# A two-layer graph kernel whose edge loops run 5 iterations of 500 groups in place of 25 iterations of 100

## The chip, the cores and the metric

The kernel runs on one core of one Trainium2 chip. The metric is the device time in microseconds (us); lower is better. The time given for the kernel before is the median of three runs. A profile is one further execution, recorded instruction by instruction; it is slower than the timed runs, and its own time is given beside theirs.

The engines are named as the profile names them: PE (matrix multiplies, with PEld for its weight loads), DVE (vector), ACT (scalar activations and copies), POOL (here almost only the issuing of indirect DMAs), SP (issues plain DMAs).

## What is computed

There are 30,000 nodes of 128 numbers and 960,000 edges, sorted by destination. Layer 0 normalises the nodes, then applies two relational graph convolutions with 32 edge types made of 8 basis matrices; layer 1 normalises again and applies a gated convolution with 4 edge types.

```python
h = relu(layernorm(x))                      # layer 0
def rel_graph_conv(h, basis, coeff, bias):  # W_r = sum_b coeff[r, b] * basis[b]
    msg = (h @ W)[src, etype32] * edge_weight
    return segment_sum(msg, dst) + bias
x = x + rel_graph_conv(relu(rel_graph_conv(h, 1)), 2)

h = relu(layernorm(x))                      # layer 1
for t in range(4):
    k, q, v = h @ Wk[t] + bk[t], h @ Wq[t] + bq[t], h @ Wv[t] + bv[t]
    msg = where(etype4 == t, sigmoid(k[dst] + q[src]) * v[src], 0)
    outs[t] = segment_sum(msg, dst) + h @ Ws[t] + b[t]
x = x + mean(outs)
```

## The kernel before

**Preparation (lines 187 to 290).** Twenty-five steps of 1,200 nodes (`STEPS`) compute `h0`, the normalised nodes. `load(i)` fetches rows on SP; `statistics(i)` takes ten means and variances on DVE, then the square root on ACT and, back on DVE, the reciprocal and the shift; `results(i)` applies them in ten ACT instructions and stores. In the loop (lines 266 to 270) the statistics of step i+1 stand ahead of the results of step i. Between them goes one piece of `edge_chunk`, which turns destinations into positions within a window and looks for positions out of range; `even` and `late` (lines 280 to 286) test that the edges of a group do not reach nodes that a node step has yet to finish. If anything fails, `any_path`, a general and unsorted version, is run instead of `sorted_path`.

**Three passes over the edges (`edge_pass`, lines 342 to 381).** `c1` and `c2` are the two relational convolutions (`rel_body`), `g` is the gated one (`gate_body`). The unit of work is a group of 384 edges (G = 3 tiles of 128), whose destinations fall into a window of 32 nodes; S = 5 groups are a step; SB = 5 steps share one set of index loads (`loads(k)`), whose number per iteration is NQ. There are 2,500 groups. `NI` iterations of `NG` groups, 25 of 100, are the turns of a hardware loop; the body of an iteration is written out in full. The loop is of the kind "staggered": the engines do not meet at its end but may run on into the next stage, and the body is cut by `tc.stage_boundary()` into four stages (every 25 groups), with `leave_stage()` two steps into each one.

**A group of `c1` and `c2`.** POOL issues three indirect gathers (line 118, called in line 523), each of 128 rows, into `hg`, which has five buffers: POOL can be five groups, 15 gathers, ahead of PE. DVE makes `hits` once a step and `sb` once a group (line 527). PE multiplies `hg` by `sb` into `pa` (line 531) and ACT copies `pa` into `ab` (line 535). After a step `bases_out` (line 486) multiplies `ab` by the eight basis matrices into `pb`, and `add_windows` (line 414) adds the result to the resident array `agg` on DVE, two steps later. In `c1` the coefficients come from `types`, `onehot` (line 451 on DVE, line 456 on PE) and `coefficients` (line 466), which are made two steps and one step ahead; the first ones of an iteration are made at its start, before its first group (lines 496 to 500), and the last two steps are finished after its last group (lines 549 to 551).

**A group of `g`.** POOL gathers three tiles into `qv` (ten buffers: 30 gathers ahead), PE looks up keys by a one-hot product into `pk` (line 588), DVE adds, ACT takes the sigmoid, DVE multiplies (`msg`, line 597), PE sums into `po` (line 599).

**Node steps (`after_first`, `after_second`, `after_third`).** When all edges of 120 nodes (VB) are done, these nodes are finished: activation, transposes, store; in `after_second` also the normalisation and the products with 12 weight matrices. A node step is a list of pairs (n, piece); step u of an iteration places a piece at group u * PERIOD + n, where `beside(n)` runs it after the group's own instructions. PERIOD is 9 before, so the pieces move by one place within the five groups of a step from one node step to the next. LAG = 480 nodes are not yet finished when the loop ends; four node steps after each pass, interleaved, finish them (lines 375 to 381).

**Codes.** In `c1`, once an iteration, `codes` (lines 785 to 815) computes the indices that pass `g` will use: four loads on SP, three DVE instructions, two stores on ACT.

The order of instructions on each engine is the order of the program text; nothing is rearranged.

Of the kernel before, what the change touches and what calls it, by code (L numbers as in the profile page):

```python
# [9 lines left out]
F32 = mybir.dt.float32  # L10
I32 = mybir.dt.int32
BF16 = mybir.dt.bfloat16
# [23 lines left out]
NGR = NT // G  # L36
S = 5
SB = 5
NQ = 4
NS = NQ * SB  # L40
NGS = S * SB
NTS = NGS * G
NG = S * NS
# [1 line left out]
NI = NGR // NG  # L45
VB = 120
NPI = N // NI
PERIOD = NG * VB // NPI - 1
LAG = 4 * VB
NX = N + LAG  # L50
LEAD = 3 * VB
GAP = 8
EPS = 1e-5
CH = 5
# [18 lines left out]
def kernel(  # L73
# [113 lines left out]
    with tc.tile_pool(name="prep", bufs=2) as prep, tc.tile_pool(name="pre", bufs=4) as pre, \  # L187
# [37 lines left out]

        def load(i):
            if i < STEPS:
                xts[i] = pre.tile([PX, KX, D], F32, name="xt")
                nc.sync.dma_start(xts[i], rows(x, i))

        def statistics(i):
            if i < STEPS:
                st = pre.tile([PX, KX, 6], F32, name="st")
                mvs[i] = pre.tile([PX, KX, 2], F32, name="mv")
                for k in range(KX):
                    nc.vector.bn_stats(st[:, k, :], xts[i][:, k, :])
                    nc.vector.bn_aggr(mvs[i][:, k, :], st[:, k, :])
                scales[i] = pre.tile([PX, KX], F32, name="rs")
                nc.scalar.activation(scales[i], mvs[i][:, :, 1], AF.Sqrt, bias=eps[:PX])
                nc.vector.reciprocal(scales[i], scales[i])  # L240
                shifts[i] = pre.tile([PX, KX], F32, name="off")
                nc.vector.scalar_tensor_tensor(shifts[i], mvs[i][:, :, 0], -1.0, scales[i],
                                               op0=ALU.mult, op1=ALU.mult)

        def results(i):
            h = pre.tile([PX, KX, D], F32, name="h")
            for k in range(KX):
                nc.scalar.activation(h[:, k, :], xts[i][:, k, :], AF.Relu,
                                     scale=scales[i][:, k:k + 1], bias=shifts[i][:, k:k + 1])
            nc.scalar.dma_start(rows(h0, i), h)  # L250
# [9 lines left out]

        with tc.manual_schedule():
            between = edge_steps()
            for i in range(3):
                load(i)
            statistics(0)
            for i in range(STEPS):
                load(i + 3)
                statistics(i + 1)
                next(between, int)()
                results(i)  # L270
            for step_ in between:
                step_()
# [62 lines left out]
    def sorted_path():  # L335

        for u in range(NPI // VB):
            late = min(g for g in range(NG)
                       if min((g // S + 2) * S + S - 2, NG) > u * PERIOD + 1)
            assert (u + 1) * VB - late * NPI // NG <= LEAD  # L340
        with ExitStack() as all_:
            def edge_pass(name, body, after, banks, extra=None):


                with ExitStack() as held:
                    weights = held.enter_context(tc.tile_pool(name=f"{name}_w", bufs=1))
                    steps, start = after(weights), body(weights)
                    with tc.tile_pool(name=f"{name}_io", bufs=NQ) as io, \
                            tc.tile_pool(name=f"{name}", bufs=2) as pool, \
                            tc.tile_pool(name=f"{name}_n", bufs=1) as npool, \  # L350
                            tc.tile_pool(name=f"{name}_nps", bufs=banks, space=PSUM) as nps, \
                            tc.tile_pool(name=f"{name}_c", bufs=1, space=PSUM) as cps, \
                            tc.tile_pool(name=f"{name}_ps", bufs=2, space=PSUM) as ps:
                        cp = cps.tile([P, 4 * D], F32, name="cp")
                        iw, ic = cp[:, :W], cp[:, W:W + 1]
                        nc.vector.tensor_copy(iw, irow)
                        nc.vector.tensor_copy(ic, icol)
                        run = start(cps)
                        with tc.For_i(0, NI, 1, iteration_sync="staggered") as i:
                            with tc.manual_schedule():  # L360
                                todo = {}
                                for n, step_ in extra(i, npool) if extra else ():
                                    todo.setdefault(n, []).append(step_)
                                for u in range(NPI // VB):
                                    at = i * -NPI + (N + LAG - (u + 1) * VB)
                                    for n, step in steps(at, npool, nps, 2):
                                        todo.setdefault(u * PERIOD + n, []).append(step)
                                assert W < TQ * 8 * B and max(todo) < NG

                                def beside(n):  # L370
                                    for step in todo.get(n, ()):
                                        step()

                                run(i, io, pool, ps, cp, iw, ic, beside)
                    left = LAG // VB
                    with tc.tile_pool(name=f"{name}_l", bufs=left) as lpool, \
                            tc.tile_pool(name=f"{name}_lps", bufs=8, space=PSUM) as lps:
                        for together in zip(*(steps(at, lpool, lps, left)
                                              for at in range(0, LAG, VB))):
                            for _, step in together:  # L380
                                step()
# [34 lines left out]
            def rel_body(table, weights, second):  # L416
# [13 lines left out]
                def body(bas, pos, hits, i, io, pool, ps, cp, iw, ic, beside):  # L430
# [70 lines left out]
                    for s in range(NS):  # L501
                        k = s // SB
                        if s % SB == 0:
                            if s:
                                tc.stage_boundary()
                            if k + 1 < NQ:
                                loads(k + 1)
                        if s % SB == 2:
                            leave_stage()
                        idx, relc, start = stage[k][:3]  # L510
                        if s + 2 < NS:
# [42 lines left out]
            def gate_body(i, io, pool, ps, cp, iw, ic, beside):  # L554
# [54 lines left out]
                for n in range(NG):  # L609
                    s, g, k = n // S, n % S, n // NGS  # L610
                    if n % NGS == 0:
                        if n:
                            tc.stage_boundary()
                        if k + 1 < NQ:
                            loads(k + 1)
                    if g == 0 and s % SB == 2:
                        leave_stage()
                    if g == 0 and s + 1 < NS:
                        types(s + 1)
# [56 lines left out]
            def after_second(weights):  # L676
# [9 lines left out]
                def steps(at, pool, ps, deep):  # L686
# [63 lines left out]
                    def own():  # L750
                        nc.vector.scalar_tensor_tensor(cols, xs, bsc, got["po"], op0=ALU.add,
                                                       op1=ALU.add)

                    return ((1, copy), (2, rows_), (3, stats), (4, norm_), (5, turn), (6, relu),
                            (7, weight(0)), (7, weight(1)),
                            (8, biased(0, kt)), (8, biased(1, qvt[:, :, :D])),
                            (8, weight(2)), (8, part),
                            (9, biased(2, qvt[:, :, D:])), (9, own), (9, store(knode, kt)),
                            (10, store(qvnode, qvt)))
                return steps  # L760

            def after_third(weights):
# [21 lines left out]

            def codes(i, pool):

                dr, er, kr = (pool.tile([NG, GE], t, name=n) for n, t in (
                    ("dr", I32), ("er_row", I32), ("kr", F32)))
                kc = pool.tile([NG, GE], BF16, name="kc")
                sx, ex = (pool.tile([TP, NQ * NTS], I32, name=n) for n in ("sx", "ex"))  # L790
                cols = ds(i * (NQ * NTS), NQ * NTS)

                def rows(array):
                    return bass.AP(tensor=array.tensor, offset=i * (NG * GE),
                                   ap=[[GE, NG], [1, GE]])

                def load():
                    nc.sync.dma_start(dr, rows(dst_row))
                    nc.sync.dma_start(er, rows(et4_row))
                    nc.sync.dma_start(sx, src[:, cols])  # L800
                    nc.sync.dma_start(ex, et4[:, cols])

                def less():
                    nc.vector.tensor_tensor(kr, dr, dr[:, 0:1].to_broadcast([NG, GE]),
                                            ALU.subtract)
                    nc.vector.scalar_tensor_tensor(sx, sx, float(T), ex, op0=ALU.mult, op1=ALU.add)

                def typed():
                    nc.vector.scalar_tensor_tensor(kc, kr, float(T), er, op0=ALU.mult, op1=ALU.add)

                def store():
                    nc.scalar.dma_start(rows(kcode), kc)
                    nc.scalar.dma_start(qidx[:, cols], sx)

                return (NGS + 1, load), (NGS + 6, less), (NGS + 7, typed), (NGS + 8, store)

            edge_pass("c1", rel_body(h0, basis[0], False), after_first, 2, codes)
            edge_pass("c2", rel_body(h1, basis[1], True), after_second, 2)
# [233 lines left out]
```

## Time and profile before

| | us |
|---|---|
| median of three timed runs (28445.0 to 28455.75) | 28447.31 |
| time of the profiled execution | 33838.86 |
| its span, first to last instruction | 33837.1 |
| POOL busy in it | 21296.4 |
| PE busy | 19734.2 |
| PE weight loads busy | 16782.1 |
| DVE busy | 11542.2 |
| ACT busy | 3644.4 |

In the profiled execution the first gather of `c1` starts at 169.48 us, that of `c2` at 11314.35, that of `g` at 22339.68, and the last one of all at 33805.12. The mean granted clock of PE is 0.681 of full speed over the span. A line of the profile's list of groups reads: line of the code, engine, operation, output and inputs, count, then the busy time in us and the mean ns of one, then the idle time of the engine just ahead of these instructions and what ended it. A line of a timeline reads: start in us, length in us, engine, line, operation, and in brackets the idle time before it and what ended that.

### The profile page before, as it was taken

What the parts mean: (1) busy time and instruction counts of PE and PEld (TensorE: products, weight loads), DVE (VectorE), ACT (ScalarE), POOL (GpSimd) and SP (SyncE); (2) the same over time, 40 slices, a digit from 0 to 9 for tenths busy, and PEclk for the clock granted to TensorE, in tenths of its full rate; (3) what the DMA queues carried; (4) which work ended last, traced back from release to release, by engine and by line L of the source; (5) the groups of instructions that cost most, each with busy time, mean ns of one, the idle gap of its engine ahead of it and who ended that gap; (6) DMA issues with size and microseconds to landing.
All of it is one profiled execution on the core that took longest, in us unless ns stands there. A gap on an engine that the chain in (4) does not pass through costs nothing.

```text
span 33837.1 us, 297715 instructions
## 1 busy us (share of the span) xinstructions
PE 19734.2 (58%) x83304; PEld 16782.1 (50%) x83304; DVE 11542.2 (34%) x23695; ACT 3644.4 (11%) x9834; POOL 21296.4 (63%) x22514
## 2 busy tenths in 40 slices
PE   4555555555555555665566565655555555555555
PEld 3444444444444444444444444445555555555555
DVE  3333333333333333333333333333333333333333
ACT  1000000000000111111111111111111111111111
POOL 5666666666666666666666666666666666666665
PEclk8777777777777777777777777765555555555555
DMA  3222222222222222222222222234444444444444
GB/s 102 66 65 64 65 64 66 65 65 65 65 65 64 65 65 66 66 65 65 65 65 66 65 65 65 65 103 124 124 124 124 124 124 125 124 124 124 125 124 120
DMA packets 1973054, 2913.52 MB, mean 86 GB/s; under 512 B 678765, under 2 KB 1355881, under 8 KB 1971545
## 3 DMA queue, kind: packets, MB, share of 16 engines
q0 software_dynamic: 840000, 1967.52, 21.4%
q1 hardware_dynamic: 725347, 651.17, 6.4%
q10 hardware_dynamic: 406197, 276.11, 2.9%
q8 instruction: 777, 12.73, 0.2%
q14 instruction: 733, 6.00, 0.1%
HBM read 2618.79 MB, written 274.16 MB: 85 GB/s over the span
## 4 chain that ended last, share of the span: by engine, by line


## 5 line engine op out<-in xcount | busy, mean ns | idle before, releaser
L118 POOL DMA_INDIRECT hg<-h,idx x15000 | 14175.6, 945 | 8092.4 <-issue 4258.4
L531 PE MATMUL pa<-sb,hg 128*128 128x256 f32 x30000 | 9232.2, 464 | 6808.7 <-issue 5685.1
L531 PEld LDWEIGHTS pa<-sb,hg 128*128 128x128 f32 x30000 | 6848.7, 238 | 8712.6 <-issue 6423.5
L118 POOL DMA_INDIRECT qv<-qvtab,qi x7500 | 7093.9, 946 | 4416.4 <-issue 2291.4
L599 PE MATMUL po<-sel,msg 128*128 128x32 f32 x15000 | 3449.8, 386 | 4592.3 <-DVE msg L597 3790.8
L599 PEld LDWEIGHTS po<-sel,msg 128*128 128x128 f32 x15000 | 3410.6, 327 | 4881.1 <-DVE msg L597 3957.9
L527 DVE TENSOR_TENSOR sb<-hits,ce 128x768 f32<-128x768 f32 x5000 | 4597.1, 949 | 541.7 <-issue 221.1
L588 PE MATMUL pk<-kw,oh 128*128 128x128 f32 x15000 | 3960.9, 437 | 183.7 <-issue 160.3
L535 ACT COPY ab<-pa 128x256 f32<-128x256 f32 x5000 | 1811.3, 373 | 19679.2 <-remote 9114.6
L629 DVE TENSOR_TENSOR pk<-pk,qv 128x384 f32<-128x384 f32 x2500 | 1405.8, 562 | 7052.6 <-remote 5162.6
L414 DVE TENSOR_TENSOR agg<-agg,pb 128x32 f32 x5000 | 939.9, 188 | 8030.9 <-remote 5411.6
L588 PEld LDWEIGHTS pk<-kw,oh 128*128 128x128 f32 x15000 | 3455.1, 330 | 186.4 <-issue 186.4
L486 PE MATMUL pb<-ab,bas 128*128 128x160 f32 x16000 | 2399.7, 304 | 118.1 <-ACT ab L535 68.6
L486 PEld LDWEIGHTS pb<-ab,bas 128*128 128x128 f32 x16000 | 2341.2, 194 | 216.6 <-ACT ab L535 100.4
L630 ACT ACTIVATE pk<-pk 128x384 f32<-128x384 f32 x2500 | 1185.3, 475 | 9393.4 <-DVE pk L629 6008.0
L726 PE MATMUL bank<-wall,hT 128*120 128x512 f32 x1524 | 1019.5, 791 | 961.1 <-DVE kt L737 411.6
L597 DVE TENSOR_TENSOR msg<-pk,qv 128x384 f32<-128x384 f32 x2500 | 1364.7, 547 | 0.0
L515 DVE TENSOR_TENSOR hits<-cp,relc 128x480 f32<-128x480 f32 x1000 | 663.8, 664 | 1310.3 <-remote 786.4
L575 DVE TENSOR_TENSOR oh<-kb,cp 128x1920 f32<-128x1920 bf16 x500 | 1071.9, 2144 | 90.6 <-issue 74.7
L726 PEld LDWEIGHTS bank<-wall,hT 128*120 128x120 f32 x1524 | 339.2, 239 | 1264.3 <-issue 549.0
L456 PE MATMUL cp<-coeff,oh 128*128 128x64 f32 x4000 | 658.1, 305 | 513.2 <-issue 350.2
L456 PEld LDWEIGHTS cp<-coeff,oh 128*128 128x128 f32 x4000 | 657.6, 229 | 549.0 <-issue 483.4
(79 smaller groups left out, 4039.9 us busy)
## 6 DMA issues: line engine op xcount, KB each, us to landing
hg<-h,idx POOLq DMA_INDIRECT x15000
kb<-kcode SPq DMA_DIRECT2D x500, 480.0 KB
kw<-ktab SPq DMA_DIRECT2D x2500, 64.0 KB
er<-in_et_row SPq DMA_DIRECT2D x500, 256.0 KB
qvtab<-qvt ACTq DMA_DIRECT2D x254, 480.0 KB
qv<-qvtab,qi POOLq DMA_INDIRECT x7500
ktab<-kt ACTq DMA_DIRECT2D x254, 240.0 KB
ce<-ce ACTq DMA_DIRECT2D x500, 60.0 KB
```

The lines of the kernel that those rows point to most:

```text
L118: nc.gpsimd.indirect_dma_start(out=to, out_offset=None, in_=table, in_offset=bass.IndirectOffsetOnAxis(ap=idx, axis=0))
L456: nc.tensor.matmul(pc[s][:, c].rearrange("p q l b -> p (q l b)"), lhsT=oh[s][:, c, :], rhs=coeff.rearrange("p q l b -> p (q l b)"), start= ...
L486: nc.tensor.matmul(po[s].rearrange("p s w -> p (s w)"), lhsT=bas[:, b, :], rhs=ab[s][:, b].rearrange("p s w -> p (s w)"), start=(b == 0), ...
L527: nc.vector.tensor_mul(sb, hits[:, of, :].unsqueeze(2).to_broadcast([TP, G, B, W]), ce[s][:, of, :].unsqueeze(3).to_broadcast([TP, G, B, W]))
L531: nc.tensor.matmul(pa.rearrange("p b w -> p (b w)"), lhsT=hg[:, j, :], rhs=sb[:, j].rearrange("p b w -> p (b w)"), start=(j == 0), stop=(j ...
L535: nc.scalar.copy(ab[s][:, :, g, :], pa)
L588: nc.tensor.matmul(pk[n][:, j, :], lhsT=oh[n // S][:, n % S, j * TP:(j + 1) * TP], rhs=kw[n], start=True, stop=True)
L597: nc.vector.tensor_mul(msg, pk[n], qv[n][:, :, 1, :])
L599: nc.tensor.matmul(po[s][:, g, :], lhsT=msg[:, j, :], rhs=sel[s][:, g * G + j, :], start=(j == 0), stop=(j == G - 1))
L629: nc.vector.tensor_add(pk[n], pk[n], qv[n][:, :, 0, :])
L630: nc.scalar.activation(pk[n], pk[n], AF.Sigmoid)
L726: nc.tensor.matmul(bank(a, VB, T * D), lhsT=hT, rhs=wall[:, a].rearrange("p t f -> p (t f)"), start=True, stop=True)
```

## The change

The number of index sets per iteration, NQ, goes from 4 to 20. This makes an iteration 500 groups long and leaves 5 of them; the stage boundaries, which stood at every index set, now stand at every fifth (every 125 groups), and the buffers of the index loads stay at four by number. PERIOD becomes 10, the node steps of `after_second` start with piece 0 in place of 1, LAG goes from 480 to 360 nodes and LEAD from 360 to 240 (the tested bound N + LAG - LEAD - W stays the same). The preparation takes statistics two steps ahead and splits off the square root, the reciprocal and the shift as `scale(i)`, one step ahead; `xt` has five buffers in place of four, `h` three in place of four. `codes` works in four parts of 125 groups per iteration, ten groups apart, through the same buffers.

```diff
-NQ = 4
+NQ = 20
 NS = NQ * SB
+BEGINS = [NQ // 4 * q for q in range(1, 4)]
...
-PERIOD = NG * VB // NPI - 1
-LAG = 4 * VB
+PERIOD = NG * VB // NPI
+LAG = 3 * VB
...
-LEAD = 3 * VB
+LEAD = 2 * VB
...
-                xts[i] = pre.tile([PX, KX, D], F32, name="xt")
+                xts[i] = pre.tile([PX, KX, D], F32, name="xt", bufs=5)
...
+        def scale(i):
+            if i < STEPS:
                 scales[i] = pre.tile([PX, KX], F32, name="rs")
                 nc.scalar.activation(scales[i], mvs[i][:, :, 1], AF.Sqrt, bias=eps[:PX])
                 nc.vector.reciprocal(scales[i], scales[i])
...
-            for i in range(3):
+            for i in range(4):
                 load(i)
             statistics(0)
+            scale(0)
+            statistics(1)
             for i in range(STEPS):
-                load(i + 3)
-                statistics(i + 1)
+                load(i + 4)
+                statistics(i + 2)
+                scale(i + 1)
                 next(between, int)()
                 results(i)
...
-                    with tc.tile_pool(name=f"{name}_io", bufs=NQ) as io, \
+                    with tc.tile_pool(name=f"{name}_io", bufs=4) as io, \
...
                         if s % SB == 0:
-                            if s:
+                            if k in BEGINS:
                                 tc.stage_boundary()
...
-                        if s % SB == 2:
+                        if s % SB == 2 and k in (0, *BEGINS):
                             leave_stage()
...
-                    return ((1, copy), (2, rows_), (3, stats), (4, norm_), (5, turn), (6, relu),
-                            (7, weight(0)), (7, weight(1)),
+                    return ((0, copy), (1, rows_), (2, stats), (3, norm_), (4, turn), (5, relu),
+                            (6, weight(0)), (6, weight(1)),
...
-                return (NGS + 1, load), (NGS + 6, less), (NGS + 7, typed), (NGS + 8, store)
+                    at = NGS + 1 + h * 10
+                    return (at, load), (at + 5, less), (at + 6, typed), (at + 7, store)
+
+                return [step_ for h in range(4) for step_ in part(h)]
```

`gate_body` gets the same two conditions on `stage_boundary` and `leave_stage`.

## The prediction

> **What bounds the kernel now.** I read the page first, then POOL's timeline, then the turn from one iteration to the next on all engines, then the ends of the passes and the waits of the preparation.
>
> The page's head and its two largest rows:
>
> ```profile
> span 33837.1 us, 297715 instructions
> ...
> PE 19734.2 (58%) x83304; PEld 16782.1 (50%) x83304; DVE 11542.2 (34%) x23695; ACT 3644.4 (11%) x9834; POOL 21296.4 (63%) x22514
> ...
> L118 POOL DMA_INDIRECT hg<-h,idx x15000 | 14175.6, 945 | 8092.4 <-issue 4258.4
> ...
> L118 POOL DMA_INDIRECT qv<-qvtab,qi x7500 | 7093.9, 946 | 4416.4 <-issue 2291.4
> ```
>
> POOL issues 22,500 gathers and is the busiest engine, though only at 63%. What it does in the rest is told by its timeline in the first iteration of `c1`:
>
> ```profile
> 213.64 0.94 POOL L118 DMA_INDIRECT hg<-h,idx  x1 [0.30 <-issue]
> 214.89 0.94 POOL L118 DMA_INDIRECT hg<-h,idx  x1 [0.30 <-DMA hg<-h,idx]
> 216.14 0.94 POOL L118 DMA_INDIRECT hg<-h,idx  x1 [0.30 <-issue]
> 217.38 0.94 POOL L118 DMA_INDIRECT hg<-h,idx  x1 [0.30 <-issue]
> 221.56 0.94 POOL L118 DMA_INDIRECT hg<-h,idx  x1 [3.24 <-PE pa L531]
> ```
>
> A gather takes 0.945 us and follows the last one after 0.30 us more: a pitch of 1.25 us, at which POOL waits for nobody; then, once in 15 gathers, it waits some 3 us for PE. Over all start times of POOL's timeline, 20,200 of the 22,499 intervals are below 1.26 us, with a mean of 1.2493; the other 2,299 hold 5,526 us beyond 1.25 each.
>
> Now the step that decides my numbers: the timed runs take 28,447.3 us, the profiled one 33,838.9, 5,391.5 more. If the pitch is the same without recording, the timed run is made of 22,500 x 1.2493 = 28,109 us of gathers, 169.5 before the first one, 35.3 and 43.6 between the passes (11277.81 to 11314.35 and 22294.80 to 22339.68, less one pitch), 32.0 after the last, and 1.8 outside the span: 28,391. **That leaves 56 us for all stalls inside the passes**, where the profile has 5,447. So nearly all the stalls seen in the profile belong to the recording. PE fits that: counting PE's records in the timelines, they come at 5.3, 5.0 and 5.6 per us in `c1`, `c2`, `g`, almost one rate for three different bodies, and readers of `pa` start up to 8 us after PE's recorded ends (ACT at 4611.23, the product recorded up to 4603.24).
>
> The turn of an iteration in `c1`:
>
> ```profile
> 4613.15 2.90 PE L531 MATMUL pa<-sb,hg 128*128 128x256 f32 x6 [9.91 <-issue]
> ...
> 4616.51 2.97 PE L486 MATMUL pb<-ab,bas 128*128 128x160 f32 x16 [0.46 <-ACT ab L535]
> ...
> 4621.80 2.19 DVE L414 TENSOR_TENSOR agg<-agg,pb 128x32 f32 x10 [8.75 <-remote]
> ...
> 4625.10 0.49 DVE L451 TENSOR_SCALAR oh<-er,icol 128x512 f32<-128x512 int32 x1 [1.11 <-issue]
> ...
> 4630.72 0.67 DVE L515 TENSOR_TENSOR hits<-cp,relc 128x480 f32<-128x480 f32 x1 [2.06 <-PE cp L456]
> ...
> 4632.43 8.24 PE L531 MATMUL pa<-sb,hg 128*128 128x256 f32 x24 [1.75 <-DVE sb L527]
> ...
> 4635.63 0.94 POOL L118 DMA_INDIRECT hg<-h,idx  x1 [12.76 <-PE pa L531]
> ```
>
> The old iteration's last products, its last additions, and the new iteration's one-hots and coefficients stand in one chain; from the end of the last group's product (4616.05) to the next group's (4632.43) PE takes in no gathered row for 16.4 us, and POOL, five groups ahead, stops. From POOL's starts, the step with this stop is longer than the others by 9.0 us in `c1` (30.8 against 21.8), 3.6 in `c2`, 3.6 in `g`.
>
> Ends of passes and preparation (timelines; waits of DVE up to 170 us):
>
> ```profile
> 11280.36 1.17 PE L531 MATMUL pa<-sb,hg 128*128 128x256 f32 x2 [0.59 <-DMA hg<-h,idx]
> ...
> 11314.35 0.94 POOL L118 DMA_INDIRECT hg<-h,idx  x1 [35.60 <-DMA idx<-in_src]
> ```
>
> ```profile
> 22314.97 12.61 PE L726 MATMUL bank<-wall,hT 128*120 128x512 f32 x24
> ```
>
> ```profile
> DVE rs L240 <- ACT rs L239: 10.1, 25, 1.0
> ```
>
> **What the Trainium skill says.** "Perfetto Trace Analysis", section "DMA Instruction — SWDGE (GPSIMD)": the recorded end of such a DMA is the end of descriptor generation, not of the data's movement. The trace agrees: the last gather of `c1` starts at 11277.81, is over at 11278.75, and its product starts at 11280.36, on a DMA. The same page, "Summary: the profiler window per engine type", calls a matmul's end an estimate; here line 414 starts 2.3 us after the recorded end of line 486. "NOTIFIC — the notification-queue block", section 3, says that record keeping can hold an engine back when an internal FIFO fills. No run here shows a FIFO; the near-constant record rate fits. "TensorE: Matmul & The Clock Gate", Part 1, has the PE clock either whole or halved; the trace's mean of 0.681 is a mixture of these, so my chain below could be shorter at full clock.
>
> **The change part by part.**
>
> *Iteration turns.* 25 become 5 in each pass: 20 fewer of each. In `c1` without recording: call T the start of an iteration's last gather. Its product starts at T+2.6 (11280.36 - 11277.81) and ends at T+3.0 with records of 0.38 us, at T+3.7 as recorded there; 16.4 us of chain; 3.2 us until the first new group is through and frees its buffer (4632.43 to 4635.63): T+22.6 to T+23.3. POOL wants that buffer for its 16th gather, at T+20.0. So a turn costs 2.6 to 3.3 us, or nothing if the clock is whole (line 486 then takes half). The 56 us left over, divided by 24 turns, are 2.3: I take 2.3, and 20 x 2.3 = **46 us** saved, between 0 and 56. In `c2` the chain has no one-hots: the same stretch runs there from 15717.73 to 15728.60, 10.9 us, so T+17.1 to T+17.8 stays under T+20: 0. In `g`, POOL is 30 gathers (37.5 us) ahead and the turn takes some 16 to 20 us: 0. If a shorter pitch takes this cover away, `c2` would show first.
>
> *Stage boundaries.* 75 inner ones per pass become 15. POOL's gap there in `c1` is 1.55, 1.43 and 1.83 us in place of 1.25, in `c2` 1.25: at most 27 us by the profile, and part of the same 56: not counted again.
>
> *Preparation.* DVE is the bound there: its busy share is 0.88 between 100 and 140 us, and 10.1 us of its gaps are waits for the square root. With statistics two ahead, the root is long done; ACT's last results follow 8 us behind DVE as before. The DMAs are at 0.73 to 0.87 of their time from 20 to 140 us and may take some back. I take **-9**, between -3 and -11. The square root's later place in ACT's queue is behind `results`, 3.9 us, covered by DVE's 3.95 us of statistics; were it not, the old wait would return.
>
> *Three leftover node steps for four.* `c2`: 6 of the 24 products, 12.61/4 = 3.2 us, and about 0.3 of line 747: -3.5. `c1`: one DMA issue (2.77/4) and its share of copies: -1. `g`: -1. Together **-5.5**, between -2 and -8.
>
> *Codes.* 20 parts for 25: DVE has 20 x about 1.6 us in place of 25 x 1.56; four loads on SP and two stores on ACT's queue each time, on SP's queue ahead of the loads of `er` for two steps later. A part's loads wait for the stores of the part before, issued three groups (11 us) earlier. Everything is under POOL's pitch: 0. Uncovered it could hold `er` up by a few us, 20 times: +40 at most.
>
> *Node steps every tenth group.* The same instructions, now always at the same groups of every second step: 0, covered by POOL's lead (18.75 us less the 7 us or so in which a group is gathered, lands and is multiplied, which leaves 12). The cost without cover is the second rival.
>
> Sum: -46 - 9 - 5.5 = -60.5 on the timed runs. On the profiled execution's own time: 20 x (9.0 + 3.6 + 3.6) = 324 and 15, so 33,839 - 339 = 33,500, if recording stalls stay as they are. I carry over to the median only what fits into its 56 us: **28,387**.
>
> **Rivals.**
>
> *The turns cost in the timed runs what they cost in the profile.* The pitch would be shorter without recording, (28,447 - 283 - 405)/22,500 = 1.234 us, with 405 us of stalls left to remove from. For: the issue gap of 0.30 us may contain recording. Against: a 1.2493 mean that hits the total within 56 us. Time: 28,447 - 324 - 15 = 28,108; part of it, 28,110 to 28,300.
>
> *Node steps in lock step make it slower.* PERIOD = 10 is two steps, so in `c2` two of the weight products (each two records of 0.79 us) always come at the group of `bases_out`: some 2.6 + 4.6 + 3.2 = 10.4 us of PE at a halved clock in one group, against some 12 us of lead. It decides when PE falls more than 12 us behind: then each of 250 node steps stalls POOL. At 1 us each, +250 - 60: 28,637. For: no other alignment relieves it. Against: before, one node step in five has it already, and the longest mean step of `c2` outside the turn is 1.5 us above the mean.
>
> *All hidden.* The turns fit under POOL's lead and the 56 us lie elsewhere: only -14.5, 28,433.
>
> **How the numbers follow.** Forecast 28,387, 52%, own range 28,350 to 28,420; turns as in the profile, wholly or in part, 18%; hidden 18%; lock step 12%. A measurement of this kernel can tell about 0.2%, 57 us, so the line is 28,390: of the forecast's 52% about 35 lie below it. Faster 0.35 + 0.18 = 0.53, same 0.17 + 0.18 = 0.35, slower 0.12. The range 28,150 to 28,450 leaves out the slow case and the far end of the first rival.
>
> **What would show it.** In the changed kernel's profile: the pitch still 1.25; one 12 us stop of POOL per 500 groups in `c1`; first gather near 160 us; the gap before `g` near 40 us in place of 43.9; the wait of line 240 for ACT gone. A steady stall every tenth group would prove the lock step; a timed gain above 100 us would prove the pitch argument wrong.

## The result, and the profile after

In 20 timed runs of each kernel beside one another, before takes 28,446.6 us (28,436.7 to 28,456.0) and the changed kernel 28,400.7 us (28,392.7 to 28,406.5): 46 us less, a ratio of 0.9984 with a 95% interval of 0.9977 to 0.9990. The forecast was 28,387 us.

The page of the changed kernel, its head and the two rows of gathers:

```profile
span 28403.8 us, 286432 instructions
...
PE 21359.2 (75%) x83291; PEld 16435.5 (58%) x83291; DVE 11553.3 (41%) x23672; ACT 3642.1 (13%) x9806; POOL 21292.1 (75%) x22514
...
L119 POOL DMA_INDIRECT hg<-h,idx x15000 | 14174.7, 945 | 4770.9 <-issue 3814.5
...
L119 POOL DMA_INDIRECT qv<-qvtab,qi x7500 | 7090.1, 945 | 2321.5 <-issue 2076.5
```

The span is 28,403.8 us, so this profiled execution is no slower than the timed runs; that a profile is slower, as the part ahead of the prediction has it, was so for the one profile at hand there. The prediction had expected some 33,500 us here. The two profiles shown so far can't be subtracted, therefore: the 5,400 us between them are mostly not the change. The idle time ahead of the `hg` gathers falls from 8,092 to 4,771 us; of that, 15,000 times the 0.30 us between two gathers make some 4,500.

On one chip, called the first below (experiments 1 and 3 and half of experiment 2), before takes about 34,260 us in its timed runs too, and on the other chips from 28,443 to 28,470; each kernel is compared with before on its own chip only. A second profile of before, from one of the others, is what the profile of after is to be read against. Its head, and its `hg` row from the list of groups with the releasers in order:

```profile
span 28445.1 us, 297715 instructions
...
L118 POOL DMA_INDIRECT hg<-h,idx x15000 | 14173.8, 945 | 4807.3 <-issue 3884.4 <-PE pa L531 405.4 <-PE pb L486 211.7
```

Between these two, 8,092 becomes 4,807 with no change to the kernel at all. What the change removes ahead of these gathers is the small difference that remains, 4,807.3 to 4,770.9.

The places that the prediction named, from the timelines of the changed kernel and from the waits of its first 160 us (engine, line, what was waited for: us in total, times, longest):

```profile
160.83 1.10 POOL L119 DMA_INDIRECT hg<-h,idx  x1 [132.79 <-issue]
...
9610.78 0.94 POOL L119 DMA_INDIRECT hg<-h,idx  x1 [38.03 <-issue]
...
18987.08 9.23 PE L733 MATMUL bank<-wall,hT 128*120 128x512 f32 x18
...
19009.28 0.94 POOL L119 DMA_INDIRECT qv<-qvtab,qi  x1 [35.62 <-DMA qi<-qidx]
```

```profile
DVE rs L244 <- ACT rs L243: 0.9, 1, 0.9
```

The first gather starts at 160.83 us in place of 169.5; DVE waits once for a square root, 0.9 us, in place of 25 times, 10.1. After `c2` the leftover node steps have 18 products in place of 24.

I split the span by POOL's start times: a gather every 1.2488 us where nobody is waited for (the mean of the intervals below 1.26 us, the same in both kernels), and what lies beyond that, by place; gathers of an iteration are counted from 0 here, so the one of the prediction's stop has the number 15. Two profiles of the changed kernel (the one above, and the last run of this study) against the second profile of before, in us:

| place | before | after | after, again |
|---|---|---|---|
| start to first gather | 169.7 | 160.8 | 160.9 |
| `c1`, gathers 10 to 18 of an iteration | 29.7 | 3.0 | 4.3 |
| `c1`, all the rest beyond the pitch | 51.4 | 46.9 | 39.8 |
| last gather of `c1` to first of `c2` | 34.0 | 39.0 | 37.3 |
| `c2`, beyond the pitch | 1.4 | 1.3 | 1.8 |
| last gather of `c2` to first of `g` | 40.6 | 36.6 | 37.4 |
| `g`, beyond the pitch | 2.1 | 1.7 | 0.7 |
| last gather to end | 21.1 | 19.5 | 19.7 |
| change of the sum | | -41.2 | -48.1 |

Two terms make most of it: some 26 us at the turns of `c1`, 9 in the preparation. The rest of `c1` gains 5 to 12 us, the gap before `g` 3 to 4, and the gap before `c2` gives 3 to 5 back: the two gaps and the end together are 95.7 us before, 95.1 and 94.4 after.

### The profile page after: what moved, and what is told of

It reads as the page before. It is cut to its first block, busy times and chain, and to the rows that moved or that the text cites. A ratio compares the mean times of both kernels' runs of the same rounds, so it can differ in the third digit from the quotient of the medians.

```text
span 28403.8 us, 286432 instructions
## 1 busy us (share of the span) xinstructions
PE 21359.2 (75%) x83291; PEld 16435.5 (58%) x83291; DVE 11553.3 (41%) x23672; ACT 3642.1 (13%) x9806; POOL 21292.1 (75%) x22514
## 5 line engine op out<-in xcount | busy, mean ns | idle before, releaser
L119 POOL DMA_INDIRECT hg<-h,idx x15000 | 14174.7, 945 | 4770.9 <-issue 3814.5
L538 PE MATMUL pa<-sb,hg 128*128 128x256 f32 x30000 | 10018.9, 455 | 4541.0 <-DMA hg<-h,idx 3713.7
L538 PEld LDWEIGHTS pa<-sb,hg 128*128 128x128 f32 x30000 | 5587.5, 212 | 8351.5 <-DMA hg<-h,idx 5081.3
L606 PE MATMUL po<-sel,msg 128*128 128x32 f32 x15000 | 3635.3, 399 | 2226.5 <-DVE msg L604 2221.4
L595 PE MATMUL pk<-kw,oh 128*128 128x128 f32 x15000 | 4024.5, 442 | 37.7 <-DVE oh L582 37.7
L493 PEld LDWEIGHTS pb<-ab,bas 128*128 128x128 f32 x16000 | 3375.6, 265 | 157.5 <-ACT ab L542 8.8
L493 PE MATMUL pb<-ab,bas 128*128 128x160 f32 x16000 | 3336.5, 381 | 4.6 <-ACT ab L542 4.6
L744 DVE TENSOR_TENSOR kt<-bank,ball 120x512 f32<-120x512 f32 x253 | 175.0, 692 | 2996.2 <-PE bank L733 2996.2
L716 DVE BATCH_NORM_STATS2 st<-bank 120x6 f32<-120x128 f32 x253 | 75.6, 299 | 2326.4 <-PE bank L713 2326.4
L733 PE MATMUL bank<-wall,hT 128*120 128x512 f32 x1518 | 738.0, 595 | 0.0
L463 PEld LDWEIGHTS cp<-coeff,oh 128*128 128x128 f32 x4000 | 542.6, 197 | 89.9 <-issue 56.9
```

The source lines that it names most:

```text
L119: nc.gpsimd.indirect_dma_start(out=to, out_offset=None, in_=table, in_offset=bass.IndirectOffsetOnAxis(ap=idx, axis=0))
L493: nc.tensor.matmul(po[s].rearrange("p s w -> p (s w)"), lhsT=bas[:, b, :], rhs=ab[s][:, b].rearrange("p s w -> p (s w)"), start=(b == 0), ...
L538: nc.tensor.matmul(pa.rearrange("p b w -> p (b w)"), lhsT=hg[:, j, :], rhs=sb[:, j].rearrange("p b w -> p (b w)"), start=(j == 0), stop=(j ...
L595: nc.tensor.matmul(pk[n][:, j, :], lhsT=oh[n // S][:, n % S, j * TP:(j + 1) * TP], rhs=kw[n], start=True, stop=True)
L606: nc.tensor.matmul(po[s][:, g, :], lhsT=msg[:, j, :], rhs=sel[s][:, g * G + j, :], start=(j == 0), stop=(j == G - 1))
```

## The experiments

**1. The kernel before again, on the first chip.** No edit.

> The kernel before, unchanged, recorded once more. Theory A (pitch of a gather fixed at 1.249 us, turns of an iteration in c1 cost some 1 to 2 us each): if this recording holds the engines back less, its span is near 28,445, the pitch is 1.249, the first gather starts at 169.5, and POOL's stops above 1.26 us within the passes add up to 60 to 75 us, most of them at the 16th gather of an iteration of c1. Theory B (turns are fully hidden): the stops are 50 us as in the changed kernel, none of them at the 16th gather, and the gain lies ahead of, between and after the passes. If it is held back as before (span near 33,800), it tells neither.

Measured: 34,227.1 us profiled, and 34,260.5 us as the median of 25 timed runs on the same chip. So the slow figure is not the recording. The pitch of a gather is 1.2513 us there, all but unchanged; 5,873 us lie beyond it (1,872 in `c1`, 1,717 in `c2`, 2,208 in `g`, the rest in the gaps between the passes). What differs is PE. The list of waits of this run:

```profile
ACT ab L535 <- remote: 9208.8, 1011, 33.1
ACT ab L535 <- PE pa L531: 8265.3, 2309, 21.5
...
POOL hg L118 <- remote: 2589.1, 909, 4.6
```

and of the second profile of before:

```profile
ACT ab L535 <- PE pa L531: 16154.6, 4925, 27.0
```

There ACT finds the end of PE's product 4,925 times in 5,000, and starts 0.04 us after it in the mean. On the first chip the releaser is given as "remote" 1,011 times, where the trace has no fitting event, and the copy starts 3.8 us after the recorded end in the mean: as far as its readers tell, PE completes later than its recorded ends say. In the profile that the prediction was made from the same lag is 3.6 us. On which chip it was taken is not known; by this lag it is of the same kind.

**2. The number of iterations undone, on both kinds of chip.** The changed kernel with 25 iterations of 100 groups.

```diff
-NQ = 20
+NQ = 4
```

and `codes` as it was before.

> The changed kernel with 25 iterations of 100 groups again (NQ = 4, codes in one part an iteration); preparation, PERIOD 10, LAG and LEAD as changed. Theory A: 20 turns more in each pass, 20 x 1.5 = +31 us on the changed kernel, so near 28,431 (ratio to before 0.9995). Theory B: turns are hidden, so near 28,401 (0.9984).

> The changed kernel with 25 iterations of 100 groups and the codes of before; only the number of turns and the codes differ from the change. If before takes about 28,447 us here: theory A (turns of c1 cost 1 to 3 us each) 28,425 to 28,447; theory B (turns hidden, the gain is in the ends and the preparation) 28,400 to 28,412. If before takes about 34,260 us here: 34,235 as in the earlier run.

Measured on the first chip: 34,234.6 us, ratio 0.9991 (0.9984 to 0.9997), 26 us below before. On a chip where before takes 28,445.3: 28,428.9, ratio 0.9994 (0.9986 to 1.0002), 16 us below before. The full change gains 46 us, so the turns and the `codes` that go with them are worth about 30 us there. The profile of the second run shows where: 22.9 us at gathers 10 to 18 of `c1`'s iterations, against 3.0 and 4.3 with five iterations, and some 54 us in the rest of `c1`, against 46.9 and 39.8. The turns of `c1` are thus worth 19 to 20 us against this profile, 25 to 27 against that of before.

**3. Two other parts undone, on the first chip.** The preparation of before (the part of the edit that is in the loop):

```diff
-                load(i + 4)
-                statistics(i + 2)
-                scale(i + 1)
+                load(i + 3)
+                statistics(i + 1)
```

and, in another kernel, the leftover nodes:

```diff
-LAG = 3 * VB
+LAG = 4 * VB
-LEAD = 2 * VB
+LEAD = 3 * VB
```

> The changed kernel with the preparation of before (statistics one step ahead, root and reciprocal with them). Both theories: the first gather at 169.5 in place of 160.8, so +9 us: 28,410 (0.9987). If the earlier end of the preparation were eaten by later waits: 28,401.

> The changed kernel with LAG at 480 nodes and LEAD at 360, so four leftover node steps after each pass and not three. Theory A: +5.5 us, 28,406 (0.9986), of which 3.5 between c2 and g. Theory B: the ends of the passes carry most of the gain: +15 to +20 us, 28,418 (0.999).

Measured: 33,656.5 us, ratio 0.9822 (0.9808 to 0.9835), and 33,666.2 us, ratio 0.9822 (0.9809 to 0.9836). Both are some 600 us below before. With the 25 iterations of experiment 2 this gain was 26 us, so on this chip nearly the whole worth of these two kernels is in the 20 turns that each pass no longer has: (34,234.6 - 33,660) / 60 = 9.6 us a turn. With the old preparation the first gather starts at 170.8 us, without it at 161.2: 9.6 us on this chip, 8.9 in the table.

The stops inside the iterations stay. In the run with the old preparation 5,291 us lie beyond the pitch in the three passes; with 25 iterations (experiment 2) it is 5,897, and in before 5,797, at a pitch of 1.2513 in place of 1.2487 us. Of the 606 us that the 25 iterations add, 370 lie in `c2` and `g`, which have no `codes`: it is the turns that make most of it. The `hg` rows of before and of the run with the old preparation:

```profile
L118 POOL DMA_INDIRECT hg<-h,idx x15000 | 14197.6, 947 | 8326.5 <-issue 4265.4 <-remote 2589.1 <-PE pa L531 1047.8
```

```profile
L119 POOL DMA_INDIRECT hg<-h,idx x15000 | 14156.7, 944 | 7963.0 <-issue 4095.4 <-remote 2506.1 <-PE pa L532 648.9
```

Why does a turn of `c1` cost over ten us there (13.0 us at gathers 10 to 18 of before, 312.7 / 24) and one or so elsewhere, with almost the same chain of work? My reading, which no run tests by itself: POOL's cover of 15 gathers exists only while PE is caught up. On the first chip PE is the late one all the time, POOL already stands at its limit when the turn begins, and a turn is paid in full.

**4. The kernel before, where it takes 28,447 us.** No edit.

> The kernel before once more, for a profile. If before takes about 28,447 us here: the pitch of a gather 1.249 us in all three passes, at most 60 us beyond it inside the passes, ACT's copies starting within 0.2 us of the recorded end of PE's product. Theory A (turns of c1): 24 stops at the 16th gather of an iteration of c1, of 1 to 3 us each. Theory B (ends): no stop there above 0.5 us, and the change's 46 us are in the preparation (9), the gaps between the passes and the end (27) and other places. If before takes about 34,260 us here: about 5,870 us beyond the pitch, as in the first run of it, and copies 3.7 us late.

Measured: 28,447.0 us profiled, 28,445.3 timed. Recording costs nothing that can be seen here. In the timeline of its turn into the fourth iteration of `c1`:

```profile
1303.71 0.70 PE L531 MATMUL pa<-sb,hg 128*128 128x256 f32 x2 [0.56 <-DMA hg<-h,idx]
...
1304.87 4.11 PE L486 MATMUL pb<-ab,bas 128*128 128x160 f32 x16 [0.46 <-ACT ab L535]
...
1319.79 6.51 PE L531 MATMUL pa<-sb,hg 128*128 128x256 f32 x16 [1.75 <-DVE sb L527]
...
1322.99 0.94 POOL L118 DMA_INDIRECT hg<-h,idx  x1 [2.24 <-PE pa L531]
```

The iteration's last gather started at T = 1301.08. Its product ends at T+3.3, the chain of the turn takes 15.4 us (1304.41 to 1319.79), and the first buffer is free at T+21.9. POOL wanted it at T+20.0 (16 times 1.2488): a stop of 1.9 us here, 29.7 / 24 = 1.2 in the mean. Theory A holds: the stops are there, at the 16th gather. Of the 24 turns 11 show a stop there of 1.4 to 2.7 us, the other 13 one of at most 0.6. What parts them is the time of the 16 products of line 486: 3.5 to 4.6 us in the 11 turns, 2.44 us in each of the 13.

The turn after 500 groups in the changed kernel is the same chain; there the 16 products (now line 493) ran at the faster of two speeds:

```profile
2045.29 0.70 PE L538 MATMUL pa<-sb,hg 128*128 128x256 f32 x2 [0.72 <-DMA hg<-h,idx]
...
2046.45 2.44 PE L493 MATMUL pb<-ab,bas 128*128 128x160 f32 x16 [0.46 <-ACT ab L542]
...
2052.64 0.49 DVE L458 TENSOR_SCALAR oh<-er,icol 128x512 f32<-128x512 int32 x1 [1.51 <-issue]
...
2060.07 4.27 PE L538 MATMUL pa<-sb,hg 128*128 128x256 f32 x12 [1.75 <-DVE sb L534]
...
2063.27 0.94 POOL L119 DMA_INDIRECT hg<-h,idx  x1 [0.99 <-PE pa L538]
```

The chain is 14.1 us (2045.99 to 2060.07) and POOL's stop 0.7 us. What the prediction took from the Trainium skill, "TensorE: Matmul & The Clock Gate", Part 1 (the clock is whole or halved), agrees with the trace in that there are two speeds: most of these products take either 0.30 or 0.47 us each, and some turns have both. The ratio is 1.6, so they don't show a halving. The chain is longer by just the time that the products lose (15.3 to 15.4 us where they take 4.11, 13.4 to 13.6 in most of the turns where they take 2.44), so their speed decides which turns stop POOL.

**5. One buffer fewer, in the kernel before.** POOL's cover becomes 12 gathers.

```diff
-                            hg = pool.tile([TP, G, D], F32, name="hg", bufs=5)
+                            hg = pool.tile([TP, G, D], F32, name="hg", bufs=4)
```

> The kernel before with four hg buffers for five: POOL may be 12 gathers ahead of PE in place of 15, so a turn that just exceeds the cover costs 3.75 us more. If before takes about 28,447 us here: theory A (turns of c1 at the edge of the cover, those of c2 2 to 3 us under it) +90 us in c1 and +24 x 1 to 2 us in c2, 28,560 to 28,590; theory B (turns well hidden) at most +40, below 28,490. If before takes about 34,260 us here: +90 us in c1 and +90 in c2 from the turns alone, 34,440, and more if the stops inside the iterations grow too.

Measured: 28,609.5 us, ratio 1.0059 (1.0044 to 1.0074), 164 us more, and over the 28,590 at which Theory A's range ended, which had too little for `c2`. The stops move to the 13th gather. A turn of `c1` and one of `c2`:

```profile
567.45 0.94 POOL L118 DMA_INDIRECT hg<-h,idx  x1 [5.98 <-PE pa L531]
...
10123.86 0.94 POOL L118 DMA_INDIRECT hg<-h,idx  x1 [2.82 <-PE pa L531]
```

In `c1` they are 114.9 us over 24 turns, 4.8 each; with five buffers they were 1.2, and three gathers' pitch is 3.75: 4.95 was to be expected. In `c2` they are 73.7 us, 3.1 each, where with five there were none. So `c1`'s turn frees a buffer at about T+21.0 and `c2`'s at T+19.3: `c1` is 1 us over the edge of the cover, `c2` 0.7 us inside it. This is the run that shows the mechanism of the prediction with its size.

**6. One buffer more, in the changed kernel.**

```diff
-                            hg = pool.tile([TP, G, D], F32, name="hg", bufs=5)
+                            hg = pool.tile([TP, G, D], F32, name="hg", bufs=6)
```

> The changed kernel with six hg buffers for five: POOL may be 18 gathers ahead of PE in place of 15. If before takes about 28,447 us here: theory A (what is left beyond the pitch in c1, 50 us, is POOL running out of buffers) 28,355 us; rival (these stops are late landings or a late index load, which no buffer covers) 28,395. If before takes about 34,260 us here: 33,660 if PE itself is too slow there (a buffer shifts its stops and saves at most 3.75 us a turn, 35 us in all), below 33,000 if it is a matter of lead.

Measured: 28,412.4 us beside 28,445.3 of before, ratio 0.9989 (0.9982 to 0.9995); not better than five buffers. My 28,355 was wrong. The stop at the 16th gather is gone (0.2 us left), but 41.3 us remain in `c1`, 7.7 of them at gathers 49 to 62 (the next experiment), and `c2` has new stops at the very first gather of an iteration, 8.9 us in all. One of them:

```profile
11473.98 0.94 POOL L119 DMA_INDIRECT hg<-h,idx  x1 [1.97 <-DMA hg<-h,idx]
```

Five divides 500 and six doesn't: an iteration begins with buffer 0 again, which group 498 has used just before. In all four stops the gather starts 1.38 to 1.39 us after the recorded end of group 498's product. `c1`, with the same six buffers, has no stop there, because that product ends 1.5 to 1.7 us before the gather is due. I did not try a number that divides.

**7. What is left in `c1`: the loads of `codes`.** In the changed kernel the view of the DMA queues between 2105 and 2120 us, in 40 slices (the digits are tenths), with the issues in it:

```profile
DMA  2015005443239387799999493373222253016006
...
er<-in_et_row SPq DMA_DIRECT2D x1, 256.0 KB
hg<-h,idx POOLq DMA_INDIRECT x12
dr<-in_dst_row SPq DMA_DIRECT2D x1, 187.5 KB
er_row<-in_et_row SPq DMA_DIRECT2D x1, 187.5 KB
sx<-in_src SPq DMA_DIRECT2D x1, 187.5 KB
ex<-in_et SPq DMA_DIRECT2D x1, 187.5 KB
```

and in the timeline of the same stretch:

```profile
2113.00 0.50 PEld L538 LDWEIGHTS pa<-sb,hg 128*128 128x128 f32 x2 [4.22 <-DMA hg<-h,idx]
...
2115.57 0.94 POOL L119 DMA_INDIRECT hg<-h,idx  x1 [1.41 <-issue]
```

In eight neighbouring slices, 3 us, the DMA engines are at 70% and more, with 1 MB of plain loads beside the gathers; gathered rows land late, PE's weight load waits 4.2 us for them, and POOL is idle for 1.4 us in place of 0.3. At gathers 49 to 62 of an iteration 30.1 us are lost over the 25 iterations of before, 7.6 and 8.0 over the five of the changed kernel, where only the first of an iteration's four parts falls on them. Two kernels tested this. The first runs `codes` in `c2`:

```diff
-            edge_pass("c1", rel_body(h0, basis[0], False), after_first, 2, codes)
-            edge_pass("c2", rel_body(h1, basis[1], True), after_second, 2)
+            edge_pass("c1", rel_body(h0, basis[0], False), after_first, 2)
+            edge_pass("c2", rel_body(h1, basis[1], True), after_second, 2, codes)
```

> The changed kernel with codes run in c2 in place of c1; the same instructions, 20 parts, in another pass. Theory C (the four loads of a part, 0.75 MB at once beside the 0.25 MB of er, make gathers land late, and these are most of c1's 50 us beyond the pitch; c2 has no er loads and so has room): c1 falls to about 20 us beyond the pitch, c2 stays below 8, 28,370 us. Rival (it is the amount of the four loads alone): c2 gets the 30 us that c1 loses, 28,400. If before takes about 34,260 us here: 33,630 or 33,660.

The second leaves it in `c1`, with the four loads of a part five groups apart and the parts 30 groups apart (the part of the edit that places them):

```diff
-                    at = NGS + 1 + h * 10
-                    return (at, load), (at + 5, less), (at + 6, typed), (at + 7, store)
+                    at = NGS + 1 + h * 30
+                    return ((at, load(dr, rows(dst_row))), (at + 5, load(er, rows(et4_row))),
+                            (at + 10, load(sx, src[:, cols])), (at + 15, load(ex, et4[:, cols])),
+                            (at + 20, less), (at + 21, typed), (at + 22, store))
```

> The changed kernel with the four loads of a part of codes five groups apart in place of back to back, and the parts 30 groups apart. Theory C (loads in one burst): no stop at groups 18 and 19, c1 about 25 us beyond the pitch, 28,375 us. Rival (any load of 187.5 KB beside an er load holds the gathers up): the stops are spread out, c1 stays near 50 us, 28,400. If before takes about 34,260 us here: 33,630 or 33,660.

Measured, with `codes` in `c2`: 28,423.4 us where before takes 28,470.0, ratio 0.9984 (0.9977 to 0.9991); beyond the pitch 31.5 us in `c1` and 9.0 in `c2`. With the loads apart: 28,431.3, ratio 0.9986 (0.9980 to 0.9993), 48.1 us in `c1`. So the stops do come from `codes` (out of `c1`, and those at gathers 49 to 62 fall from 8 to 0.4 us), but the burst is not what counts: spread out, the same bytes cost about the same in sum, as far as one profile can tell where two of the changed kernel differ by 6 us. `codes` costs `c1` 9 to 17 us in the changed kernel (39.8 and 46.9 less 30.4, each without the turns), half of what Theory C had, and `c2` pays 8 of it. The profiled span with `codes` in `c2` is 28,393.0 us, against 28,403.8 and 28,397.2: at most 11 us better, which the timed ratios can't tell from the change itself.

**8. LAG 480 again, where before takes 28,470 us.** The edit of experiment 3.

> The changed kernel with LAG 480 and LEAD 360, four leftover node steps after each pass in place of three. The prediction has 5.5 us for this (2 to 8): 28,406 us if before takes about 28,447 here, of which 3.5 in the gap between c2 and g. Rival (the loads of the next pass, which do not depend on these steps, set the gaps): under 2 us, 28,401. If before takes about 34,260 us here: 33,666 as in the earlier run.

Measured: 28,441.1 us, ratio 0.9989 (0.9983 to 0.9996). In this run the pitch is 1.2502 us, which alone is 31 us over 22,500 gathers, so I read only the gaps: from `c2` to `g` 42.0 us in place of 36.6 and 37.4, after the last gather 21.1 in place of 19.5 and 19.7, from `c1` to `c2` 36.4 in place of 39.0 and 37.3. In sum the fourth step costs 4.4 or 5.1 us, nearly all of it before `g`: nearer to the prediction's 5.5 than to the rival's 2. One profile of a kernel scatters by as much, however. In all the profiles from chips where before takes 28,443 to 28,470, the two gaps and the end are 95.7 to 99.5 us in the three with LAG 480 and 92.7 to 95.1 in the six with 360, 4.4 us apart in the mean. The timed runs can't settle it: 29 us below before, where the change itself gained 46 and 43 on other chips, with an interval of 18 us either way.

**9. The change itself once more.**

> The changed kernel itself, once more, beside before. If before takes 28,440 to 28,475 us here: theory A (25 us from the turns of c1, 9 from the preparation, 5 from the leftover node steps, some from codes) 40 to 50 us below it, 0.14 to 0.18%, and in the profile 3 to 8 us lost at the 16th gathers of c1's iterations; rival (what the first comparison showed was the chip, not the kernel) anything outside 25 to 65 us. If before takes about 34,260 us here: 33,630 to 33,670, as the two variants of it did there.

Measured: 28,400.8 us in 21 runs where before takes 28,443.5, ratio 0.9984 (0.9978 to 0.9991): 43 us, and 4.3 us at the 16th gathers. The profile of this run is the last column of the table. The change itself was not timed on the first chip; its two variants of experiment 3 stand for it there.

## Why the prediction was right, and where not

The forecast was 14 us below the measured time, within its own range. It was in favour of faster by more than 0.2%, and the change is worth 0.16%. That it came so near is in part luck: the turns gave 19 to 27 us in place of 46 and the leftover steps 5 at most, while the rest of `c1`, put at nothing, gave 5 to 12.

- **Pitch and bound.** Right. POOL's gathers set the time at 1.2488 us each (1.2493 in the prediction), and what lies beyond the pitch inside the passes is 84.6 us in before, where the prediction's remainder was 56: it had taken the pitch, the gaps and the end from its profile, which made them 11, 7 and 11 us too long.
- **"Nearly all the stalls seen in the profile belong to the recording."** This step is false. Without the recording before takes 34,260 us on the first chip (experiment 1), and with it 28,447 elsewhere (experiment 4). The stalls go with a late PE on that chip, and the prediction's profile has the same late PE. The number drawn from the step, that the timed runs have almost none of these stalls, was right all the same, since it came from the sum of the timed run and not from their cause. The near-constant rate of records, for which I had brought in the Trainium skill's "NOTIFIC — the notification-queue block", section 3, was no evidence: where no stall is seen the records come faster (5.8, 5.4 and 6.4 per us in stretches of the three passes, against 4.9, 4.6 and 5.2 in experiment 1, matrix multiplies and weight loads counted), and the same recording runs at both rates.
- **Turns, -46.** Right in place and mechanism, too large in size; this is the term that was mis-sized. I had put the whole remainder of 56 us on the turns, 2.3 us for each. The measured stop is 1.2 us in the mean, the gain 26 us (19 to 20 by experiment 2), and the one stop per 500 groups, which I had put at 12 us in a profile, is below 3. The buffer comes free at about T+21, where I had T+22.6 to T+23.3, taken from a chain of 16.4 us on a PE that was late; it is 15.4 and 14.1 in the turns shown. The rest of the remainder was `codes` and small stops. For `c2` I had T+17.1 to T+17.8 and zero cost; T+19.3 was measured, still zero, but with 0.7 us to spare.
- **Preparation, -9.** Right: -8.9. The square root's later place in ACT's queue did no harm.
- **Leftover steps, -5.5.** Near in size by experiment 8, 4.4 to 5.1, but hardly there in the table, where the gaps and the end gain 0.6 and 1.3 us in sum. The gap from `c1` to `c2`, for which I had -1, grew by 3 to 5 us. It is 35.6 us in experiment 2 and between 34.3 and 39.0 in the other kernels with LAG 360, so part of this is scatter between executions; what made it in the changed kernel stays open.
- **Codes, 0.** Wrong: it is not hidden, its loads delay gathers, and the change makes this cheaper. In before 30.1 us are lost at gathers 49 to 62, where these loads run; in the changed kernel all of `codes` costs `c1` 9 to 17 us. That would be a gain of 13 to 21 us. The other small stops of `c1` took part of it back, from some 21 us in before to some 30 (by the run with `codes` in `c2`), so that the rest of `c1` gains only 5 to 12. That the 30.1 us of before are all due to `codes` was not tested in that kernel, and what the other stops are stays open.
- **Node steps in lock step, 0.** Right, and the slower rival falls: `c2` has 1.3 us beyond the pitch in the whole pass.
- **"Turns cost in the timed runs what they cost in the profile."** False where the timing was made, true on the first chip, where the variants gain 600 us: there even 9.6 us a turn in the mean of the passes, against the (9.0 + 3.6 + 3.6) / 3 = 5.4 that I had summed from one step each. The stops go on after that step while PE catches up.

Open is why PE is late on the first chip. Its mean clock is lower there (0.678 against 0.730), but at the same 0.51 in a stretch of `g` (24,000 to 28,000 us) it gets through 5.2 records per us against 6.4, so the clock alone doesn't explain it. The runs there were all made together, so whether it is the chip or a state that it was in is not shown either.

## What to carry to other kernels

When the time of a profiled execution is far from the timed runs, first build the timed run from the profile's bound (gathers times pitch, plus ends): what is left over limits what can be gained from stalls, whatever the profile shows of them. Don't give the whole remainder to the one mechanism you know. How far one engine runs ahead is a budget in us, and taking one buffer away shows how much of it is left: here it put `c1` 1 us over the edge and `c2` 0.7 us inside.

## What the runs showed of the hardware that was not expected

- The same kernel takes 28,443 to 28,470 us on some chips and 34,260 on another, at the same pitch of POOL (1.25 us), while PE's products there reach their reader 3.8 us in the mean after their recorded ends (0.04 us elsewhere). The change is worth 0.16% on the one kind; two variants of it gained 1.8% on the other.
- The same 16 products took from 2.44 to 4.63 us in the 24 turns of one profile. The turns with 2.44 us held POOL for at most 0.6 us, those with 3.49 us and more for 1.4 to 2.7.
- On one chip the pitch of a gather was 1.2488 us in two profiles and 1.2502 in a third, and the timed runs of before lay around 28,470 after a first one of 28,441: 0.1% from a source that no record shows.
- Plain loads of 0.75 to 1 MB beside indirect gathers of 128 rows delay the gathers (PE waited 4.2 us for one), and spacing the loads out didn't make them cheaper in sum (48 us beyond the pitch in `c1`, against 44 and 50).
